# First block prepared in two token halves, loads in order of use, a third buffer of quantised activations, and the condition products two tiles later

## The chip, the cores and the metric

The kernel runs on one core of one Trainium2 chip. The metric is the device time of one execution in microseconds (us), median of the runs, lower is better. TensorE (PE) multiplies matrices, VectorE (DVE), ScalarE (ACT) and GpSimd (POOL) work on elements, and SyncE (SP) issues most of the DMA transfers. On-chip memory is SBUF; results of TensorE go to PSUM, which has eight banks of 128 x 512 fp32.

## The reference, cut to what matters

64 sequences of 64 tokens with 256 features (4096 tokens) pass through four layers, each steered by a condition vector of 64 numbers per sequence. The change touches the first layer and the preparation of the weights of the fourth.

```python
# layer 0: conditioned norm, gated GELU, ternary down product on quantised activations
scale = cond @ norm_w.T + 1.0
h = x * (scale[:, None, :] * rsqrt(mean(x * x) + EPS))
val, gate = split(h @ up_w.T)                 # 256 -> 2 x 1024
h = val * gelu(gate)
hq = clip(round(h * 127 / max|h|), -128, 127) / (127 / max|h|)   # per token
x = hq @ ternary(down_w).T + x                # 1024 -> 256
# layer 1: attention (16 heads) and SwiGLU, ada-rmsnorm with gamma, beta, alpha from cond
# layer 2: layernorm plus tanh(cond @ lin_w.T + lin_b)
# layer 3: low-rank adapter; its matrices are made for each sequence:
dWd = (h_lang @ Wdd.T + bdd) * 0.1            # 64 -> 128 x 256 per sequence
dWu = (h_lang @ Wdu.T + bdu) * 0.1
x = x + relu(x @ (Wd + dWd).T + bd) @ (Wu + dWu).T + bu
```

## The kernel before

The tokens are worked in 8 blocks of T = 512, each of TT = 4 tiles of 128 tokens. A product of fp32 precision is made of three TensorE products of high and low parts (`mm3`, L81 to L85): hi x hi, hi x lo, lo x hi. A "split" makes the high part on ScalarE (a rounding copy, L222 for x, L322 for the weights) and the low part on VectorE (L223, L326).

**Layer 0** runs in `l0`, a loop over n, the tile number. In iteration n stand: `upper(n, 0)` and `upper(n, 1)`, each 12 products of 128 x 512 for the two halves of the hidden features, followed by gelu on ScalarE (`g`, L408) and the gate product on VectorE (`h`, L409); then `quant(n)` on VectorE (L415 to L420: maximum, scale, round, write the bf16 tile `q`), a transpose of `q` to `qt` by a DMA on the SP queue (L422), and `lower(n - 3)`: eight bf16 products with the ternary weights (L434) and the residual sum on VectorE (`x`, L435). The tiles `q` have two buffers, `qt` four.

**The generated matrices** of layer 3 are made in the same loop. At n = 5, 8, 11, 15, 18, 22, 25 and 29 four pieces are made: `gen_load` brings a 512 KB piece of weights (`gt`, SP queue), `gen_make` multiplies it (L278), `gen_stage` copies two PSUM banks to an SBUF tile (`stg`, ScalarE, L291), `gen_store` sends it to DRAM from the POOL queue (L298). The staging tiles alternate between the pools "a" and "kv", two in each.

**Block preparation.** `prep_load(i)` loads x of block i feature-major (`xf`) and token-major (`xt`), `prep_parts(i)` scales it by the condition (`xs`, L371) and splits it (`xhl`, `xll`), `prep_scale(i)` makes the root of the mean square: squares on ScalarE (L215), the root on POOL (L206 to L208). For block i+1 these stand at the block's first, second and third tile.

**The start.** Up weights come in four pieces `upst0` to `upst3`. `warm` lets TensorE transpose an identity matrix while the loads run. The first products are those of tiles 0 and 1 with the weight pieces 2 and 0 (`first`, 24 products), in the order of the tiles.

**The other condition products.** `cond_norm` makes layer 0's scale at the start. The rest are made by two hooks: `cond_load` (the loads `cwt`, `vc`, `bo`) and `cond_rest` (an iota on POOL, 28 products L152 and 4 products L156, 14 VectorE instructions L138 to L170, two tanh on ScalarE, a store to `alphad`). Hooks of iteration n run after both `upper` of that iteration and, for n < 31, before `quant(n)`.

**What sets the order.** PE, ACT, DVE and POOL run in the order of the program text. The SP queue's DMAs are put in order by a scheduler. Tiles of one tag share a fixed number of buffers, and an instruction that writes a new tile waits until the old one in that buffer was read. PSUM is one ring of eight banks.

Of the kernel before, what the change touches and what calls it, by code (L numbers as in the profile page):

```python
# [8 lines left out]
F32 = mybir.dt.float32  # L9
F32R = mybir.dt.float32r  # L10
BF16 = mybir.dt.bfloat16
AF = mybir.ActivationFunctionType
ALU = mybir.AluOpType
# [4 lines left out]
P = 128  # L18
NB = 64
L = 64  # L20
D = 256
NTOK = NB * L
T = 512
NBLK = NTOK // T
BB = T // L
TT = T // P
FF = 1024
BN = 128
X1 = 5
# [3 lines left out]
V_NORM, V_AG, V_AB, V_AA, V_FG, V_FB, V_FA, V_LIN = range(8)  # L33
# [3 lines left out]
def tile_kernel(ctx: ExitStack, tc, xT, x, condT, cw, upT, downT, qkvT, woT, ghT, outT_w,  # L37
                vecs, rows, g1, g2, gb, out):
    nc = tc.nc
# [3 lines left out]
    main = ctx.enter_context(tc.tile_pool(name="main", bufs=1))  # L43
# [8 lines left out]
    pools = {}  # L52
# [7 lines left out]
    uid = [0]  # L60
# [13 lines left out]
    def block(name):  # L74
        return main.tile([P, TT, D], F32, tag="x1", bufs=X1, name=name)

    def tok(ap, i):

        return ap[i * T:(i + 1) * T, :].rearrange("(t p) d -> p t d", p=P)

    def mm3(out, l, r, first, last):  # L81

        nc.tensor.matmul(out, lhsT=l[0], rhs=r[0], start=first, stop=False)  # L83
        nc.tensor.matmul(out, lhsT=l[0], rhs=r[1], start=False, stop=False)  # L84
        nc.tensor.matmul(out, lhsT=l[1], rhs=r[0], start=False, stop=last)  # L85

    def b3(ap):
        return ap.rearrange("p (b l) -> p b l", l=L)
# [16 lines left out]
    cv = const.tile([P, 8, 2, NB], F32, name="cv")  # L105
# [1 line left out]
    w2 = const.tile([P, 2], F32, name="w2")  # L107
    par = const.tile([P, 2], F32, name="par")

    def bc(v, c, i):  # L110

        return cv[:, v, c, i * BB:(i + 1) * BB].unsqueeze(2).broadcast_to([P, BB, L])

    def cond_vector(cwv, pb, o=0):
        for c in range(2):
# [4 lines left out]
    def cond_norm():  # L120
        nc.vector.tensor_scalar(cv[:, V_NORM], cond_vector(cwn, bank("mm")), 1.0, None, ALU.add)
# [75 lines left out]
    def two(pool, name, kc, n):  # L197
        return [pool.tile([P, kc, n], F32R, name=f"{name}{k}") for k in range(2)]
# [12 lines left out]
    def rms(xb, name):  # L211
        ss = main.tile([P, TT], F32, tag="ss", bufs=2, name=f"ss{name}")
        for t in range(TT):
            junk = main.tile([P, D], F32, tag="junk", bufs=1, name=f"junk{name}_{t}")
            nc.scalar.activation(junk, xb[:, t], AF.Square, accum_out=ss[:, t:t + 1])  # L215
        return rsqrt(ss, 1.0 / D, 1e-6, name)

    def parts(name):
        return [main.tile([P, 2, T], F32R, tag=k, bufs=2, name=f"{k}{name}") for k in ("xh", "xl")]

    def split(hl, c, xs, eng=None):
        nc.scalar.copy(hl[0][:, c], xs)  # L222
        (eng or nc.vector).tensor_tensor(hl[1][:, c], xs, hl[0][:, c].bitcast(F32), ALU.subtract)  # L223
# [34 lines left out]
    GC = 512  # L258
    gen_left = [(g, sd, k) for g, sd in ((g1, s1d), (g2, s2d)) for k in range(16384 // (2 * GC))]
    gen_loaded, gen_made, gen_staged, gen_turn = [], [], [], []  # L260
# [21 lines left out]
    def gen_stage():  # L282
        if gen_made:
            pb, dst = gen_made.pop(0)
            uid[0] += 1

            gen_turn.append(pools["kv"] if len(gen_turn) % 2 else pools["a"])
            stg = gen_turn[-1].tile([P, 2, GC], F32, tag="stg" if len(gen_turn) % 2 else "qf", bufs=2,
                                    name=f"stg{uid[0]}")
            for s in range(2):  # L290
                nc.scalar.copy(stg[:, s], pb[s])  # L291
            gen_staged.append((stg, dst))
# [8 lines left out]
    def l0(hooks):  # L301
        pool = pools["a"]
        up = two(pool, "up", 2, 2 * FF)
# [3 lines left out]
        wm = sb[:, 1:2]  # L307
        blk, til = {}, {}

        ups = {}  # L310

        def load_up(j, *queues):

            js = slice(j * 512, (j + 1) * 512)
            ups[j] = main.tile([P, 2, 512], F32, tag="x1", bufs=X1, name=f"upst{j}")
            n = 2 // len(queues)
            for k, queue in enumerate(queues):
                cs = slice(k * n, (k + 1) * n)
                queue.dma_start(out=ups[j][:, cs], in_=upT.rearrange("(c p) n -> p c n", p=P)[:, cs, js])

        def half_hi(j, c):
            nc.scalar.copy(up[0][:, c, j * 512:(j + 1) * 512], ups[j][:, c])  # L322

        def half_lo(j, c):
            js = slice(j * 512, (j + 1) * 512)
            nc.vector.tensor_tensor(up[1][:, c, js], ups[j][:, c], up[0][:, c, js].bitcast(F32), ALU.subtract)  # L326
# [24 lines left out]

        def prep_load(i):
            xf = pool.tile([P, 2, T], F32, tag="xf", bufs=1, name=f"xf{i}")
            src = xT.rearrange("(c p) t -> p c t", p=P)[:, :, i * T:(i + 1) * T]
            if i == 0:
                for c in range(2):
                    nc.sync.dma_start(out=xf[:, c], in_=src[:, c])
                load_up(0, nc.sync, nc.scalar)
            else:
                nc.sync.dma_start(out=xf, in_=src)  # L360
            xt = block(f"xt{i}")
            nc.sync.dma_start(out=xt, in_=tok(x, i))
            blk[i] = [xt, xf, parts(f"l0_{i}"), None]

        def prep_parts(i):

            xf, hl = blk[i][1:3]
            xss = []
            for c in range(2):
                xs = main.tile([P, T], F32, tag="xg", bufs=2, name=f"xs{i}_{c}")  # L370
                nc.vector.tensor_tensor(b3(xs), b3(xf[:, c]), bc(V_NORM, c, i), ALU.mult)  # L371
                xss.append(xs)
            for c in range(2):
                yield
                split(hl, c, xss[c])

        def prep_scale(i):
            blk[i][1] = rms(blk[i][0], f"l0_{i}")

        def first(tiles):  # L380

            for n in tiles:
                til[n] = pool.tile([P, FF], F32, tag="h", bufs=2, name=f"h{n}")
                til[n, 0] = bank("up"), bank("up")
            for k, off in enumerate((FF, 0)):
                o = slice(off, off + 512)
                for c in range(2):
                    for n in tiles:
                        xh, xl = blk[n // TT][2]
                        ts = slice(n % TT * P, (n % TT + 1) * P)  # L390
                        mm3(til[n, 0][k], (xh[:, c, ts], xl[:, c, ts]), (up[0][:, c, o], up[1][:, c, o]), c == 0, c == 1)

        def upper(n, ch, part=None):
            i, t = divmod(n, TT)
# [17 lines left out]
        def quant(n):  # L412
            h = til[n]
            am = pool.tile([P, 4], F32, tag="am", bufs=5, name=f"am{n}")
            nc.vector.tensor_reduce(am[:, 0:1], h, AX.X, ALU.max, apply_absolute_value=True)  # L415
            nc.vector.tensor_scalar(am[:, 1:2], am[:, 0:1], 1e-5, 1.0 / 127.0, ALU.max, ALU.mult)
            nc.vector.reciprocal(am[:, 2:3], am[:, 1:2])
            nc.vector.tensor_scalar(h, h, am[:, 2:3], MAGIC, ALU.mult, ALU.add)
            q = pool.tile([P, FF], BF16, tag="q", bufs=2, name=f"q{n}")
            nc.vector.tensor_scalar(q, h, -MAGIC, 127.0, ALU.add, ALU.min)  # L420
            qt = pool.tile([P, 8, P], BF16, tag="qt", bufs=4, name=f"qt{n}")
            nc.sync.dma_start_transpose(out=qt, in_=q)  # L422
            til[n] = (am, qt)
# [16 lines left out]
        def warm(n):  # L440

            pb = bank("mm")
            for _ in range(n):
                nc.tensor.transpose(pb[:, :P], ident, ident)

        load_up(2, nc.scalar, nc.scalar)
        prep_load(0)
        nc.sync.dma_start(out=ct[64:128], in_=condT)
        load_up(3, nc.sync)
        load_up(1, nc.sync)  # L450
        til["ones"] = pool.tile([P, P], F32, name="ones")

        nc.scalar.activation(sa, nhalf[:, 0:2], AF.Gelu)
# [1 line left out]
        warm(12)  # L455
        half_hi(2, 0)
        cond_norm()
        warm(8)
        for c, _ in enumerate(prep_parts(0)):
            if c == 0:  # L460
                half_lo(2, 0)
            else:
                half_hi(2, 1)
        half_lo(2, 1)
        for c in range(2):
            half_hi(0, c)
            half_lo(0, c)
        prep_scale(0)
        first((0, 1))
        nc.vector.tensor_scalar(gl, ct, 0.1, None, ALU.mult)  # L470
        for j in (3, 1):
            for c in range(2):
                half_hi(j, c)
                half_lo(j, c)
        upper(0, 0, "rest")
        upper(1, 0, "rest")
        N = NBLK * TT
# [2 lines left out]
        for n in range(N + 2):  # L480
# [24 lines left out]
            if n == N - 1:  # L505
                quant(n)
# [430 lines left out]
    nc.gpsimd.memset(vx, 0.0)  # L937
    splits = Splitter(nc.vector, (qkv[0], qkv[1], qkvT, 2, 3 * D, 256), (wo[0], wo[1], woT, 2, D, 256))

    hooks = {3: [cond_load], 4: [cond_rest], 7: [splits.load]}  # L940
    for n in range(8, 16):
        hooks[n] = [splits.turn]
    last = NBLK * TT
# [25 lines left out]
    splits = Splitter(nc.gpsimd, (*pools["gh"], ghT, 2, 2 * FF, 512), (*pools["wout"], outT_w, 8, D, 256))  # L969
# [17 lines left out]
    for w in range(W):  # L987
        i, tp = divmod(w, 2)
# [87 lines left out]
    for n in range(5, N):  # L1076
        i, f = divmod(n, 8)
# [14 lines left out]
        up = i - 2 if more and f == 7 else i - 2 if not more and f == 0 else -1  # L1092
# [107 lines left out]
```

## Time and profile before

| | us |
|---|---|
| median of 3 runs | 771.09 (769.52 to 771.65) |
| the profiled execution | 768.89, span 767.1 |
| busy PE | 750.2 (98%) |
| busy DVE, ACT, POOL | 546.7, 396.3, 339.4 |
| moved by DMA | 118.87 MB, mean 155 GB/s |

The profile is of one execution; its times count from the start of the span. A row of the timeline gives the start, the duration, the engine, the line of the kernel, the operation, output <- inputs, the tile's shape, and in square brackets how long the engine stood idle before it and what ended that. SPq, POOLq and so on are the engines' sequencers, which issue DMAs. A row of the waits gives the sum, the number and the longest of the waits of one kind. Matmuls are pipelined, so a row's duration overlaps the next; the distance between starts is what counts. "Granted clock" is the share of full speed at which TensorE was allowed to run. A DMA's row in the timeline is its issue; its landing is later. In the chain of waits a DMA's piece runs from issue to landing.

Where the sections below speak of iteration n, these are starts in the profile of the kernel before: upper(1,1) 21.16, upper(5,0) 45.99, the generated products of n=5 48.98, upper(5,1) 52.75, upper(6,0) 56.45, upper(6,1) 59.34, upper(7,0) 62.95, upper(8,1) 76.01, upper(25,1) 207.98.

### The profile page before, as it was taken

Reading aid. Unit: us, or ns where it says so; the run is one execution under the profiler, and the core shown is the slowest. Engines: PE = TensorE matmul, PEld = TensorE weight load, DVE = VectorE, ACT = ScalarE, POOL = GpSimd, SP = SyncE. Lnnn points to the kernel's source line nnn. Section 1 sums busy time; section 2 is a strip of 40 time slices with the busy share of each in tenths; the row PEclk is TensorE's granted clock in tenths of the full one; section 3 lists DMA queues with packets and bytes.
Section 4 is the critical chain, followed back from the end, with each engine's and each line's share of the span. In section 5 each row is a group of like instructions: output and inputs, shape, how many; then the busy total and the mean of one; then the engine's idle time right before and its main releaser. Section 6 shows DMA issues by size and latency. Waiting matters only on the chain.

```text
span 767.1 us, 17409 instructions
## 1 busy us (share of the span) xinstructions
PE 750.2 (98%) x7034; PEld 618.9 (81%) x7034; DVE 546.7 (71%) x864; ACT 396.3 (52%) x818; POOL 339.4 (44%) x348
## 2 busy tenths in 40 slices
PE   8999999999899989999999999999999999999997
PEld 6866776676576878888888888888888888888886
DVE  4898777877587789998999886545555555555665
ACT  5434445435345378988878674535353434434232
POOL 2022223032224336676656417564646464545291
PEclk9999999999999999999999999999999999999999
DMA  8759998998986883555664137714180709070921
GB/s 299 200 128 255 315 279 175 334 257 191 266 211 140 184 188 88 139 143 141 157 153 110 45 125 179 165 28 112 40 181 24 197 3 218 1 192 2 232 45 56
DMA packets 117184, 118.87 MB, mean 155 GB/s; under 512 B 39616, under 2 KB 100672, under 8 KB 117104
## 3 DMA queue, kind: packets, MB, share of 16 engines
q1 hardware_dynamic: 109104, 91.55, 48.7%
q0 software_dynamic: 7488, 25.37, 10.7%
q8 instruction: 55, 0.90, 0.5%
q10 hardware_dynamic: 512, 0.85, 0.4%
q14 instruction: 25, 0.20, 0.1%
HBM read 71.41 MB, written 29.56 MB: 132 GB/s over the span
## 4 chain that ended last, share of the span: by engine, by line
PE 84%; DVE 7%; DMA 4%; issue 3%; ACT 1%; POOL 0%; SPq 0%; DVEq 0%; POOLq 0%; ACTq 0%
PE mm L83 10%; PE mm L84 10%; PE mm L85 10%; PE gh L83 7%; PE gh L84 7%; PE gh L85 7%; PE acc L83 4%; PE acc L85 4%; PE acc L84 4%; PE mm L278 3%; PE mm L434 3%; PE mm L632 2%; PE S L591 2%; PE mm L239 2%; DMA qt<-q 2%
## 5 line engine op out<-in xcount | busy, mean ns | idle before, releaser
L83 PE MATMUL mm<-up,xhl 128*128 128x512 f32 x256 | 106.4, 416 | 0.6 <-DVE h L409 0.5
L84 PE MATMUL mm<-up,xhl 128*128 128x512 f32 x256 | 103.0, 402 | 2.2 <-DVE up L326 2.2
L85 PE MATMUL mm<-up,xll 128*128 128x512 f32 x256 | 102.7, 401 | 0.0
L83 PE MATMUL gh<-xhf,gh 128*128 128x512 f32 x244 | 97.3, 399 | 0.0
L84 PE MATMUL gh<-xlf,gh 128*128 128x512 f32 x244 | 97.0, 397 | 0.0
L85 PE MATMUL gh<-xhf,gh 128*128 128x512 f32 x244 | 96.9, 397 | 0.0
L737 DVE TENSOR_TENSOR sg<-gh,sg 128x512 f32<-128x512 f32 x61 | 42.0, 688 | 77.1 <-ACT sg L736 39.9
L408 ACT ACTIVATE g<-mm,rs_l 128x512 f32<-128x512 f32 x64 | 43.7, 687 | 93.2 <-PE mm L85 60.3
L759 DVE TENSOR_TENSOR hlo<-sg,hhi 128x512 fp32r<-128x512 f32 x61 | 58.5, 959 | 31.2 <-ACT hhi L758 30.2
L758 ACT CAST hhi<-sg 128x512 fp32r<-128x512 f32 x61 | 37.8, 619 | 78.0 <-DVE sg L737 77.1
L409 DVE SCALAR_TENSOR_TENSOR h<-mm,rs_l,g 128x512 f32<-128x512 f32 x64 | 47.0, 746 | 41.8 <-PE mm L85 41.7
L83 PE MATMUL acc<-wout,hhi 128*128 128x256 f32 x256 | 75.1, 293 | 0.0
L85 PE MATMUL acc<-wout,hlo 128*128 128x256 f32 x256 | 72.7, 284 | 0.3 <-DVE hlo L759 0.2
L84 PE MATMUL acc<-wout,hhi 128*128 128x256 f32 x256 | 72.4, 283 | 0.0
L243 POOL TENSOR_TENSOR xg<-xg,cv 128x512 f32<-128x512 f32 x32 | 35.3, 1112 | 79.8 <-DVE xg L242 79.8
L83 PEld LDWEIGHTS mm<-up,xhl 128*128 128x128 f32 x256 | 49.2, 192 | 18.7 <-DVE h L409 3.6
L84 PEld LDWEIGHTS mm<-up,xhl 128*128 128x128 f32 x256 | 49.2, 192 | 12.8 <-DVE up L326 2.7
L85 PEld LDWEIGHTS mm<-up,xll 128*128 128x128 f32 x256 | 49.1, 192 | 12.2 <-DVE xll L223 0.3
L85 PEld LDWEIGHTS gh<-xhf,gh 128*128 128x128 f32 x244 | 46.1, 189 | 10.7
L84 PEld LDWEIGHTS gh<-xlf,gh 128*128 128x128 f32 x244 | 46.4, 190 | 8.1
L83 PEld LDWEIGHTS gh<-xhf,gh 128*128 128x128 f32 x244 | 46.4, 190 | 8.1
L736 ACT ACTIVATE sg<-gh 128x512 f32<-128x512 f32 x61 | 35.9, 589 | 29.2 <-PE gh L85 28.9
(189 smaller groups left out, 1886.7 us busy)
## 6 DMA issues: line engine op xcount, KB each, us to landing
gt<-in_g SPq DMA_DIRECT2D x32, 512.0 KB, 8.9
rows<-alphad SPq DMA_DIRECT2D x48, 256.0 KB, 4.3
s1d<-stg POOLq DMA_DIRECT2D x32, 256.0 KB, 9.6
s2d<-stg POOLq DMA_DIRECT2D x32, 256.0 KB, 6.6
vb<-vx SPq DMA_DIRECT2D x32, 256.0 KB, 4.6
wd<-s1d SPq DMA_DIRECT2D x32, 256.0 KB, 6.4
wu<-s2d SPq DMA_DIRECT2D x32, 256.0 KB, 6.4
xt<-in_x SPq DMA_DIRECT2D x8, 512.0 KB, 8.2
```

Source lines behind the costliest of these rows:

```text
L83: nc.tensor.matmul(out, lhsT=l[0], rhs=r[0], start=first, stop=False)
L84: nc.tensor.matmul(out, lhsT=l[0], rhs=r[1], start=False, stop=False)
L85: nc.tensor.matmul(out, lhsT=l[1], rhs=r[0], start=False, stop=last)
L243: nc.gpsimd.tensor_tensor(b3(xg), b3(xg), bc(vb, c, i), ALU.add)
L278: nc.tensor.matmul(pb[s][c * 64:(c + 1) * 64], lhsT=gl[h], rhs=gt[h, c * GC:(c + 1) * GC], start=True, stop=True, tile_position=(64 * s, 6 ...
L408: nc.scalar.activation(g, pg, AF.Gelu, scale=rs[:, t:t + 1])
L409: nc.vector.scalar_tensor_tensor(h[:, ch * 512:(ch + 1) * 512], pv, rs[:, t:t + 1], g, ALU.mult, ALU.mult)
L434: nc.tensor.matmul(py[:, :D], lhsT=qt[:, f, :], rhs=wq[:, f, :], start=f == 0, stop=f == 7)
L736: nc.scalar.activation(sg, pg, AF.Silu)
L737: nc.vector.tensor_tensor(sg, pv, sg, ALU.mult)
L758: nc.scalar.copy(h_hi, sg)
L759: nc.vector.tensor_tensor(h_lo, sg, h_hi.bitcast(F32), ALU.subtract)
```

## The change

It has three parts.

1. The start. Block 0 is loaded and prepared in two halves of 256 tokens (four sequences): the first half of both feature chunks comes first, then the weight piece `upst0`, `xt0`, `upst3`, `upst1`, and the second half of `xf`. `first` now goes by operand: for each weight piece and feature chunk, hi x hi of both tiles, then hi x lo, then lo x hi. `half_lo` of the weights stands between the low parts of x. Eight warm-up transposes become ten. The second half is prepared after weight piece 3 and before weight piece 1.
2. `cond_load` goes from n = 3 to n = 5, `cond_rest` from n = 4 to n = 6.
3. `q` gets a third buffer in pool "a". The staging tiles of pool "a" are moved to "kv": the even ones are the two halves of one 8 KB "kb" tile, the odd ones stay "qf" tiles.

On the queues this gives, as the two built programs show: SP issues after the start `xf` half 0, upst0, xt0, upst3, upst1, `xf` half 1, then the ternary weights and the `gt` as before. The two `cwt` loads were issued before the loop's sixth `gt` and now stand behind the transpose of tile 4; `bo` stands behind two more `gt` and `xf3`, as its buffer is one of block 2's `xs`. On POOL the iota stands behind block 2's root and no longer behind block 1's. In later parts of the program the order on every engine is the same.

```diff
+            k = len(gen_turn)
+            if k == 0:
+                gen_turn.append(pools["kv"].tile([P, 2, 2, GC], F32, tag="kb", bufs=2, name="stgs"))
+            else:
+                gen_turn.append(None)
+            stg = gen_turn[0][:, k // 2 % 2] if k % 2 == 0 else \
+                pools["kv"].tile([P, 2, GC], F32, tag="qf", bufs=2, name=f"stg{uid[0]}")
...
             if i == 0:
-                for c in range(2):
-                    nc.sync.dma_start(out=xf[:, c], in_=src[:, c])
-                load_up(0, nc.sync, nc.scalar)
+                H = T // 2
+                nc.sync.dma_start(out=xf[:, :, :H], in_=src[:, :, :H])
+                load_up(0, nc.sync, slice(0, 1))
+                load_up(0, nc.scalar, slice(1, 2))
+                nc.sync.dma_start(out=xt, in_=tok(x, i))
+                load_up(3, nc.sync)
+                load_up(1, nc.sync)
+                nc.sync.dma_start(out=xf[:, :, H:], in_=src[:, :, H:])
...
             for k, off in enumerate((FF, 0)):
                 o = slice(off, off + 512)
                 for c in range(2):
-                    for n in tiles:
-                        xh, xl = blk[n // TT][2]
-                        ts = slice(n % TT * P, (n % TT + 1) * P)
-                        mm3(til[n, 0][k], (xh[:, c, ts], xl[:, c, ts]), (up[0][:, c, o], up[1][:, c, o]), c == 0, c == 1)
+                    for x, w in ((0, 0), (0, 1), (1, 0)):
+                        for n in tiles:
+                            ts = slice(n % TT * P, (n % TT + 1) * P)
+                            nc.tensor.matmul(til[n, 0][k], lhsT=blk[n // TT][2][x][:, c, ts], rhs=up[w][:, c, o],
+                                             start=c + x + w == 0, stop=c + x == 2)
...
-            q = pool.tile([P, FF], BF16, tag="q", bufs=2, name=f"q{n}")
+            q = pool.tile([P, FF], BF16, tag="q", bufs=3, name=f"q{n}")
...
-        warm(8)
-        for c, _ in enumerate(prep_parts(0)):
-            if c == 0:
-                half_lo(2, 0)
-            else:
+        warm(10)
+
+        for c, _ in enumerate(prep_parts(0, slice(0, BB // 2))):
+            if c == 1:
                 half_hi(2, 1)
-        half_lo(2, 1)
+            half_lo(2, c)
         for c in range(2):
             half_hi(0, c)
             half_lo(0, c)
+        first((0, 1))
         prep_scale(0)
-        first((0, 1))
         nc.vector.tensor_scalar(gl, ct, 0.1, None, ALU.mult)
-        for j in (3, 1):
-            for c in range(2):
-                half_hi(j, c)
-                half_lo(j, c)
+        for c in range(2):
+            half_hi(3, c)
+            half_lo(3, c)
+        for _ in prep_parts(0, slice(BB // 2, BB)):
+            pass
+        for c in range(2):
+            half_hi(1, c)
+            half_lo(1, c)
...
-    hooks = {3: [cond_load], 4: [cond_rest], 7: [splits.load]}
+    hooks = {5: [cond_load], 6: [cond_rest], 7: [splits.load]}
```

More of the change, by code (lines that the diff above doesn't have):

```diff
@@ L108, in tile_kernel, with bc @@
     par = const.tile([P, 2], F32, name="par")
-    def bc(v, c, i):
-        return cv[:, v, c, i * BB:(i + 1) * BB].unsqueeze(2).broadcast_to([P, BB, L])
+    def bc(v, c, i, bs=slice(0, BB)):
+        n = bs.stop - bs.start
+        return cv[:, v, c, i * BB + bs.start:i * BB + bs.stop].unsqueeze(2).broadcast_to([P, n, L])
     def cond_vector(cwv, pb, o=0):
@@ L285, in gen_stage @@
             uid[0] += 1
-            gen_turn.append(pools["kv"] if len(gen_turn) % 2 else pools["a"])
-            stg = gen_turn[-1].tile([P, 2, GC], F32, tag="stg" if len(gen_turn) % 2 else "qf", bufs=2,
-                                    name=f"stg{uid[0]}")
+            k = len(gen_turn)
[5 more added lines that the diff above has]
+                pools["kv"].tile([P, 2, GC], F32, tag="qf", bufs=2, name=f"stg{uid[0]}")
             for s in range(2):
@@ L308, in l0, with load_up @@
         blk, til = {}, {}
[L310 to L319, printed above, removed]
+        ups, xfs = {}, {}
+        def load_up(j, queue, chunks=slice(0, 2)):
+            if j not in ups:
+                ups[j] = main.tile([P, 2, 512], F32, tag="x1", bufs=X1, name=f"upst{j}")
+            queue.dma_start(out=ups[j][:, chunks],
+                            in_=upT.rearrange("(c p) n -> p c n", p=P)[:, chunks, j * 512:(j + 1) * 512])
         def half_hi(j, c):
@@ L353, in prep_load, with prep_parts @@
             xf = pool.tile([P, 2, T], F32, tag="xf", bufs=1, name=f"xf{i}")
+            xt = block(f"xt{i}")
+            xfs[i] = xf
+            blk[i] = [xt, None, parts(f"l0_{i}"), None]
             src = xT.rearrange("(c p) t -> p c t", p=P)[:, :, i * T:(i + 1) * T]
             if i == 0:
-                for c in range(2):
-                    nc.sync.dma_start(out=xf[:, c], in_=src[:, c])
-                load_up(0, nc.sync, nc.scalar)
+                H = T // 2
[6 more added lines that the diff above has]
+                nc.sync.dma_start(out=xf[:, :, H:], in_=src[:, :, H:])
             else:
                 nc.sync.dma_start(out=xf, in_=src)
[L361 to L367, printed above, removed]
+                nc.sync.dma_start(out=xt, in_=tok(x, i))
+        def prep_parts(i, bs=slice(0, BB)):
+            xf, hl = xfs[i], blk[i][2]
+            ts = slice(bs.start * L, bs.stop * L)
             xss = []
             for c in range(2):
-                xs = main.tile([P, T], F32, tag="xg", bufs=2, name=f"xs{i}_{c}")
-                nc.vector.tensor_tensor(b3(xs), b3(xf[:, c]), bc(V_NORM, c, i), ALU.mult)
+                xs = main.tile([P, T], F32, tag="xg", bufs=2, name=f"xs{i}_{c}_{bs.start}")[:, ts]
+                nc.vector.tensor_tensor(b3(xs), b3(xf[:, c, ts]), bc(V_NORM, c, i, bs), ALU.mult)
                 xss.append(xs)
@@ L374, in prep_parts @@
                 yield
-                split(hl, c, xss[c])
+                nc.scalar.copy(hl[0][:, c, ts], xss[c])
+                nc.vector.tensor_tensor(hl[1][:, c, ts], xss[c], hl[0][:, c, ts].bitcast(F32), ALU.subtract)
         def prep_scale(i):
@@ L444, in warm @@
                 nc.tensor.transpose(pb[:, :P], ident, ident)
-        load_up(2, nc.scalar, nc.scalar)
+        for c in range(2):
+            load_up(2, nc.scalar, slice(c, c + 1))
         prep_load(0)
         nc.sync.dma_start(out=ct[64:128], in_=condT)
-        load_up(3, nc.sync)
-        load_up(1, nc.sync)
         til["ones"] = pool.tile([P, P], F32, name="ones")
@@ L467, in l0 @@
             half_lo(0, c)
+        first((0, 1))
         prep_scale(0)
-        first((0, 1))
         nc.vector.tensor_scalar(gl, ct, 0.1, None, ALU.mult)
-        for j in (3, 1):
-            for c in range(2):
-                half_hi(j, c)
-                half_lo(j, c)
+        for c in range(2):
[3 more added lines that the diff above has]
+            pass
+        for c in range(2):
+            half_hi(1, c)
+            half_lo(1, c)
         upper(0, 0, "rest")
```

## The prediction

> **What bounds the kernel now.** I read the page's first section, then the table of busy time by stretch, then the waits, and last the timeline and the chain around the two places where TensorE stands still.
>
> ```profile
> PE 750.2 (98%) x7034; PEld 618.9 (81%) x7034; DVE 546.7 (71%) x864; ACT 396.3 (52%) x818; POOL 339.4 (44%) x348
> ```
> ```profile
> 0.00:20.00 20.00, 16.41 (x56) 12.83 (x57) 9.34 (x16) 10.31 (x23) 3.85 (x11) 1.00 0.89 302
> 20.00:60.00 40.00, 39.49 (x219) 29.63 (x218) 36.56 (x71) 18.15 (x37) 6.27 (x10) 1.00 0.67 174
> 100.00:200.00 100.00, 100.00 (x536) 73.46 (x535) 75.20 (x136) 42.14 (x88) 26.43 (x41) 1.00 0.98 253
> 200.00:213.00 13.00, 11.03 (x62) 6.15 (x61) 4.01 (x10) 5.49 (x10) 2.82 (x4) 0.87 1.21 234
> ```
> Columns: stretch, length, busy PE, PEld, DVE, ACT, POOL, then granted clock, DMA share, GB/s. TensorE is the bound almost everywhere, so an edit pays only where PE stands still or runs slowly: 3.6 us missing in 0 to 20, 2.0 us in 200 to 213, and the half clock there (0.87). From 20 to 60 VectorE is full too (36.56 of 40): there PE can run ahead no further than VectorE frees PSUM banks.
>
> ```profile
> DVE q L420 <- DMA qt<-q: 3.7, 1, 3.7
> PE mm L278 <- DVE x L435: 2.9, 2, 2.0
> PE mm L84 <- DVE up L326: 2.2, 1, 2.2
> ```
> Each is (nearly) one event. The last is the start:
> ```profile
> 7.21 0.79 PE L83 MATMUL mm<-up,xhl 128*128 128x512 f32 x1
> 8.80 0.69 DVE L371 TENSOR_TENSOR xs<-xf,cv 128x512 f32<-128x512 f32 x1 [2.30 <-DMA xf<-in_xT]
> 10.15 0.80 PE L84 MATMUL mm<-up,xhl 128*128 128x512 f32 x1 [2.15 <-DVE up L326]
> 15.19 0.63 PE L83 MATMUL mm<-up,xhl 128*128 128x512 f32 x1
> 16.26 0.39 PE L83 MATMUL mm<-up,xhl 128*128 128x512 f32 x1
> 21.43 0.75 DVE L409 SCALAR_TENSOR_TENSOR h<-mm,rs_l,g 128x512 f32<-128x512 f32 x1 [2.05 <-PE mm L85]
> ```
> The first product runs at 7.21. The second needs the low part of the weights, which VectorE has queued behind the scaling of x's second chunk, and that chunk lands at 8.78. Matmuls start 0.427 us apart until 16.01 and 0.233 after. The 24 products of `first` end at 18.36.
>
> The other two waits are one stall, in the chain:
> ```profile
> 189.24 15.79 DMA qt<-q
> 205.12 0.69 DVE q L420
> 206.04 0.49 DVE x L435
> 206.58 1.47 PE mm L278 x8
> ```
> Tile 24's q needs one of two q buffers, held by tile 22's transpose, which took 15.79 us to land. VectorE waits 3.65 us; behind it in order stands L435, which frees the bank for the last generated products. PE idles 204.43 to 206.58, then runs at half clock:
> ```profile
> 208.57 0.63 PE L84 MATMUL mm<-up,xhl 128*128 128x512 f32 x1
> 210.64 0.39 PE L83 MATMUL mm<-up,xhl 128*128 128x512 f32 x1
> ```
>
> **The change part by part.** The profiled execution took 768.89 us (span 767.1, 1.8 around it), 2.2 under the median of 771.09. The steps are worked out on its trace; I subtract their sum from the median, as the waits are the program's own.
>
> *Half block first.* Before, PE had x's first chunk at 5.71. Now 256 KB with 256 tokens of both chunks come first. The Trainium skill (DMA: Bandwidth & Descriptors, "Queues, rings and completion order") says that an engine takes turns between queues packet by packet, which speaks against this: rows are now 1 KB, and the ACT queue's upst2 has 2 KB packets. In this trace a 1 KB packet takes 46 ns and a 2 KB one 84, so 16 turns of (46+84) replace 8 of (84+84): 0.74 us later, 6.45. By bytes alone it is 5.8. I take 6.2. Then scaling 256 wide 0.4 (L435, 256 wide, is 0.40 to 0.49), conversion 0.42 (ACT's 256-wide square), so PE starts near 7.1 to 7.5. The two extra warm-up transposes (0.21 each) end by 7.6 at most and fill that wait. lo(2,0) comes 1.0 us after the scaled c0 (xs c1 0.4, itself 0.6) and is wanted after two cold matmuls (0.85); no more 2.15 wait. upst0 lands near 10.2 as before and is wanted after 12 matmuls, about 12.4. So PE runs on from about 7.4.
>
> The clock rose at 16.01 and later changed at 207.16 and 210.57; all lie on a 3.413 us grid, so a step was also at 12.60. Before, the stretch 9.19 to 12.60 held idle time to 10.15; now it is full. I take 12.60: 12 matmuls at 0.427 and 12 at 0.233 from 7.4 make 15.4, against 18.36 (-2.9). If the clock still waits until 16.01, 20 cold and 4 warm end at 16.9 (-1.5). By the DMA rule (start 0.4 later) about 0.2 less.
>
> Next late: weights 1 and 3. ACT does the squares of xt0 (to 13.79), two conversions for weight 3 (1.08), two 256-wide of x's second half (0.84), two for weight 1 (1.08): 16.8, VectorE's last low part near 17.5. The second half of upper(0,1) wants it at 17.5: 0 to 0.5 us of wait. upper(1,1) begins near 18.5 (21.16 before): PE gains 2.6. VectorE's row of 21.43 comes near 19.3: it gains 2.1, having four more instructions (each 512-wide pair became four 256-wide) and a later gelu. As VectorE is full until 55.9, PE is held to about 2.0 by n=6.
>
> *Condition products from n=4 to n=6, their loads from n=3 to n=5.* The same work moves: PE 28 x L152 (2.00 us) and 4 x L156 (0.65), about 2.5 net; VectorE 14 instructions, 46.51 to 50.14, 3.63; ACT two tanh; POOL an iota and alphad's store; SP's cwt x2 (448 KB), vc, bo. PE reaches it at the end of upper(6,1): before 62.1, less 2.5 moved, less 2.0, is 57.6. The queues that it is moved past:
> ```profile
> 32.80 0.13 POOL L136 IOTA part<- 128x1 int32 x1
> 63.80 0.19 POOL L206 TENSOR_SCALAR ms_l<-ssl 128x4 f32<-128x4 f32 x1 [8.52 <-ACT junkl L215]
> 53.40 2.36 SPq L422 DMA_TRANSPOSE qt<-q  x1
> ```
> On SP, cwt now stands behind tile 4's transpose. That landed at 63.44, 14.46 us after the generated products of n=5 began (48.98). These begin near 43.4 now (less 2.5, 2.6 and a 0.5 us wait at 45.99), so it lands near 57.8; 448 KB at some 2 us per 512 KB (two gt landed 1.3 to 2.0 apart here), partly beside it, is 1.1 to 1.75: cwt at about 59. That is a new wait s at PE of about 1.4, between 0 (cwt beside the transpose) and 3. Behind it in PE's order stand lower(3) and upper(7,0), so all of PE.
>
> On POOL the iota stood after block 1's root; now it is behind block 2's, which ended at 65.10, 5.8 us after upper(6,1) began (59.34): 54.8 + 5.8 = 60.6. VectorE's 14 instructions begin with its result, 1 to 2 us after VectorE is free. bo now lies behind two gt and xf3, which before landed 4.65 us after that transpose: about 64.0 with cwt ahead; L166, 2.3 us into the 14, wants it at 62.9, a further 1.0. Behind both in VectorE's order stand quant(6) and L435 of tiles 3 and 4, which free PE's banks. From the iota: 3.63 + 1.0, quant(6) 3.1, L435 0.72, two h 1.43, quant(7) 3.04, L435 of tile 4 0.79, together 13.7: 74.3, and with the last generated bank behind it upper(8,1) at 75.2. By PE's own path it is 76.01 - 1.95 + s. Before: 76.01. So the gain left is the smaller of 0.8 and 1.95 - s: 0.55 with s at 1.4, 0.8 with 1.1, -1 with 3; with bo and iota in time 1.8. I take 0.8. A wait above 2 us would add a half-clock window (below).
>
> *Third q buffer.* q(24) then waits for tile 21's transpose, long landed, and PE first needs transpose 22 in lower(22) near 208.3, 3.3 us after it landed; 23 (landed 206.18) near 214.7. What goes is 2.15 us of PE idle. The Trainium skill (TensorE: Matmul & The Clock Gate, "Why this matters for your kernels") sets the harmful gap at over some 3 us, which would leave 2.15 alone. The trace shows a half-clock window of 3.41 us after this gap: half of it, 1.6, goes too. Sum 3.75, against 2.15 by the rule. Another view agrees: iteration 22 (same work) took 10.30 us and 25 took 14.02, 3.72 more. The trace decides: 3.7. Floor 0: transpose 22 later by over 3.3.
>
> *Staging.* Same four places in rotation, the same store to wait for; only addresses change. Attention's first use of that "kb" place follows the last store by over 20 us. I put nothing: what hides it is that ACT copies four stagings after the store; without that cover a copy waits for one store's landing (9.6 us in the page's list), against the 23 us between the visits at n=5 and n=8 (48.98 to 72.44).
>
> Sum: 0.8 + 3.7 = 4.5, profiled 764.4, median 766.6.
>
> **The rivals.** (1) cwt, iota and bo are in time: 1.8 + 3.7 = 5.5, 765.6; if VectorE holds PE back less than I think, 2.6 + 3.7 = 6.3, 764.8. For: at 20 to 60 us the DMA engines are busy 0.67 only; against: the one queue order. (2) The start's gain is used up at n=6 to 8: only the buffer is left, 767.4, or 768.9 if only 2.15 of it. (3) The third buffer doesn't pay, as transpose 22 slips or another takes its place (DMA share 0.98 in 100 to 200): 0.8 alone, 770.3. That the halves don't help (first half near 6.5, clock at 16.01) costs 1.1 to 1.4 of gain and falls in (2). (4) Slower: cwt behind a long transpose. If tile 4's, issued near 47.7 (53.40 less 3.63 and 2.1), needs 15.8 as tile 22's did, it lands at 63.5 and cwt at 65.0: PE idles 7.4, plus 1.6 of half clock, less 1.95 and 3.7: +3.35, 774.4. It decides from a wait of 6.4 us (cwt at 64.0) on; against: the same transpose took 10.04 in this trace.
>
> **How the numbers follow.** 0.3% or 2.3 us is about what a measurement of this kernel can tell from no change. Forecast 0.40, (1) 0.25, (2) 0.13, (3) 0.15, (4) 0.07. Faster: forecast, (1) and nearly all of (2), 0.75; same: (3) and a rest, 0.18; slower 0.07. The range goes from 763.8 (rival 1 with 1 us more) to 770.6 (beyond rival 3).
>
> **What would show it.** PE without a gap from 7.5, `first` ending near 15.4, clock full at 12.6; a PE wait at L152 for cwt near 57.6, and VectorE waits for the iota and for bo; upper(8,1) near 75.2; no wait at q L420 and no half clock near 205, and what follows earlier by 4 to 5 us. Wrong if L152 waits over 3 us, if lower(22) waits for its transpose, or if a new wait stands in 213 to 270, where the stretch lost 0.9 before.

## The result and the profile after

The change made the kernel slower: 773.56 us, median of 7 runs (773.14 to 775.75), against 767.58 (766.15 to 771.65) for the kernel before measured beside it, a ratio of 1.0081 with a 95% interval of 1.0058 to 1.0104. The kernel before is 3.5 us lower here than in the first three of these runs, which the prediction started from, so differences and ratios are compared below, not absolute times. The forecast was 4.5 us faster.

In the changed kernel's text the lines have moved: L152 is now L153, L420 is L432, L434 is L446, L371 is L381, the products of `first` are L402. Its busy time by stretch, with the same columns as before:

```profile
0.00:20.00 20.00, 16.49 (x62) 13.11 (x63) 8.94 (x20) 10.36 (x24) 3.85 (x11) 1.00 0.89 298
20.00:60.00 40.00, 38.73 (x191) 27.99 (x189) 36.96 (x65) 20.09 (x43) 5.80 (x8) 1.00 0.65 151
60.00:100.00 40.00, 35.43 (x188) 26.05 (x189) 23.93 (x52) 11.37 (x23) 8.80 (x15) 0.87 0.85 254
200.00:213.00 13.00, 13.00 (x77) 9.26 (x79) 10.00 (x18) 3.14 (x6) 2.71 (x5) 1.00 1.20 256
```

The hole that was at 200 to 213 (11.03 busy, clock 0.87) is closed: 13.00 of 13.00 at full clock. A new one stands at 58 to 74: TensorE has 35.43 of 40 in 60 to 100, and there the mean clock is 0.87. The start, 0 to 20, has not gained (16.49 busy against 16.41). The waits name both places:

```profile
PE mm L153 <- DMA cwt<-in_cw: 5.7, 2, 5.3
DVE gl L480 <- DMA ct<-in_condT: 2.7, 1, 2.7
```

There is no row for q L432 any more. The timeline of TensorE around the hole, and below it the chain of waits into it:

```profile
58.49 0.40 PE L85 MATMUL mm<-up,xll 128*128 128x512 f32 x1
...
64.24 0.65 PE L153 MATMUL mm<-ct,cwt 64*128 64x64 f32 x2 [5.35 <-DMA cwt<-in_cw]
65.22 3.25 PE L153 MATMUL mm<-ct,cwt 64*128 64x64 f32 x26 [0.33 <-DMA cwt<-in_cw]
68.40 1.12 PE L157 MATMUL mm<-cwt,ct 64*64 64x256 f32 x4
69.45 1.89 PE L446 MATMUL mm<-wq,qt 128*128 128x256 bf16 x8
70.99 0.78 PE L83 MATMUL mm<-up,xhl 128*128 128x512 f32 x1
```
```profile
51.94 2.42 SPq L132
54.41 10.67 DMA cwt<-in_cw
```

TensorE is done with upper(6,1) at 58.7, and the two cwt loads land at 64.1 (51.94 plus 12.2, the tile's landing time) and 65.08. The price is more than the idle time. The windows show the clock:

```profile
58.70:63.40 4.70, 0.19 (x1) 0.00 (x0) 2.68 (x10) 1.53 (x6) 1.31 (x3) 1.00 1.03 264
63.40:73.70 10.30, 9.13 (x47) 7.14 (x48) 4.96 (x13) 0.52 (x2) 0.69 (x1) 0.50 0.81 218
73.70:80.00 6.30, 6.30 (x33) 4.99 (x32) 4.14 (x7) 1.38 (x2) 2.02 (x3) 1.00 0.64 158
```

For 10.3 us TensorE had half its clock, and the small products L153, L157, lower(3) and the first of upper(7,0) fell into it. From 64.24 to upper(7,0) in the chain (71.34) are 7.1 us, where the same work takes 2.5 + 0.9 at full clock in the profile before: 3.7 lost; 71.34 to 73.7 at half clock loses 1.2. With 5.5 us of idle time the stop costs 10.4. Against this stands what the start still saves at that point, 0.9. The sum, 9.5, fits the profiles: lower(4) and what follows are 9.3 us later than before. The third q buffer takes 3.7 of these back near 204, and the profile's span is 5.2 us longer (772.3 against 767.1).

### The profile page after: what moved, and what is told of

Its sections match the earlier page's. It is cut to its first block, busy times and chain, and to the rows that moved or that the text cites. A ratio compares the mean times of both kernels' runs of the same rounds, so it can differ in the third digit from the quotient of the medians.

```text
span 772.3 us, 17418 instructions
## 1 busy us (share of the span) xinstructions
PE 752.5 (97%) x7036; PEld 620.2 (80%) x7036; DVE 547.1 (71%) x868; ACT 396.5 (51%) x820; POOL 339.3 (44%) x348
## 4 chain that ended last, share of the span: by engine, by line
PE 83%; DVE 4%; DMA 2%; issue 2%; ACT 1%; SPq 1%; POOL 0%; DVEq 0%; ACTq 0%
PE mm L83 10%; PE mm L85 9%; PE mm L84 9%; PE gh L83 7%; PE gh L84 7%; PE gh L85 7%; PE acc L83 4%; PE acc L85 4%; PE acc L84 4%; PE mm L279 3%; PE mm L446 3%; PE mm L646 2%; PE S L605 2%; PE mm L240 2%; PE mm L665 2%
## 5 line engine op out<-in xcount | busy, mean ns | idle before, releaser
L83 PE MATMUL mm<-up,xhl 128*128 128x512 f32 x248 | 102.0, 411 | 0.1
L84 PE MATMUL mm<-up,xhl 128*128 128x512 f32 x248 | 98.6, 398 | 0.2 <-DVE up L328 0.2
L85 PE MATMUL mm<-up,xll 128*128 128x512 f32 x248 | 98.4, 397 | 0.0
L420 ACT ACTIVATE g<-mm,rs_l 128x512 f32<-128x512 f32 x64 | 43.8, 688 | 93.4 <-PE mm L85 53.9
L83 PEld LDWEIGHTS mm<-up,xhl 128*128 128x128 f32 x248 | 47.1, 190 | 17.1 <-DVE x L447 1.7
L85 PEld LDWEIGHTS mm<-up,xll 128*128 128x128 f32 x248 | 46.9, 189 | 11.4
L84 PEld LDWEIGHTS mm<-up,xhl 128*128 128x128 f32 x248 | 47.0, 190 | 10.2 <-DVE up L328 0.5
```

The lines of the kernel that those rows point to most:

```text
L420: nc.scalar.activation(g, pg, AF.Gelu, scale=rs[:, t:t + 1])
```

## The experiments

First each part by itself, and the change with part 2 undone, on one chip beside the kernel before.

**The change with the condition products put back (e1).**
```diff
-    hooks = {5: [cond_load], 6: [cond_rest], 7: [splits.load]}
+    hooks = {3: [cond_load], 4: [cond_rest], 7: [splits.load]}
```


> The changed kernel with the condition products' hooks put back (load at n=3, work at n=4); the new start, the third q buffer and the moved staging stay. Theory A (the loss is part 2 alone: cwt waits on SP's queue behind tile 4's transpose): no wait at L153, the start's gain of about 2 us and the buffer's 3.7 us are left, 5 to 6 us faster than before. Theory B (the new start shifts the stores and transposes against each other, so that a long transpose hurts wherever it lies): not faster than before, a wait of several us somewhere between 45 and 100 us.

Measured: 766.78 us, ratio 0.9997 (0.9976 to 1.0017). The slowdown is gone, so it came with part 2. But 5 to 6 us were expected to be won, and nothing was: both theories missed in part. Its profile has two waits. At the start VectorE waits for ct, and in tile 18's `lower` TensorE waits for a transpose that took 18.6 us to land:

```profile
DVE gl L480 <- DMA ct<-in_condT: 3.8, 1, 3.8
PE mm L446 <- DMA qt<-q: 3.2, 1, 3.2
```

The second wait need not be in every execution: the profiled one, 770.09 us, was the slowest of the 14.

**The third buffer and the staging alone (e2)**, that is the kernel before with part 3.
```diff
-            q = pool.tile([P, FF], BF16, tag="q", bufs=2, name=f"q{n}")
+            q = pool.tile([P, FF], BF16, tag="q", bufs=3, name=f"q{n}")
...
```
The lines left out are those of the staging tiles, as in the change.

> The kernel before with only the third q buffer and the moved staging. Theory A: the wait at q L420 near 205 and the half-clock stretch behind it go, 3.7 us faster than before. Rival: transpose 22 is as late, lower(22) waits for it on TensorE, within 0.5 us of before.

Measured: 765.78 us, ratio 0.9975 (0.9959 to 0.9991), which is 1.9 us faster. In its profile the stretch 200 to 213 is full at full clock:

```profile
200.00:213.00 13.00, 13.00 (x77) 8.39 (x76) 7.62 (x15) 7.21 (x13) 2.39 (x4) 1.00 1.05 313
```

and lower(22) comes 3.9 us earlier than in the profile before. The mechanism holds; the median won only half of the 3.7 us that the one profile had shown. The kernel before ran from 764.2 to 773.6 us on this chip, and not every execution need hold that stall; that was not tested.

**The condition products alone (e3)**, that is the kernel before with the hooks at 5 and 6.
```diff
-    hooks = {3: [cond_load], 4: [cond_rest], 7: [splits.load]}
+    hooks = {5: [cond_load], 6: [cond_rest], 7: [splits.load]}
```


> The kernel before with only the condition products moved (load at n=5, work at n=6). Theory A: TensorE waits for cwt at L152 for 3 to 6 us and loses some 4 us more to half clock, 6 to 10 us slower than before, less up to 3.7 if the shift takes the stall near 205 away. Theory B (only in company with the new start): within 1 us of before.

Measured: 774.15 us, ratio 1.0103 (1.0064 to 1.0142). The same hole at the same place, without the new start and with two q buffers (whose stall, 4.4 us, is still there):

```profile
PE mm L152 <- DMA cwt<-in_cw: 5.7, 2, 5.5
DVE q L420 <- DMA qt<-q: 4.4, 1, 4.4
```

**The new start alone (e4)**, that is the change with parts 2 and 3 undone.

> The kernel before with only the new start (halves, load order, products by operand). Theory A: first ends 2 to 3 us earlier, the clock is full one 3.4 us step earlier, and about 2 us of it are left at the end; 2 us faster, if the stall near 205 stays as it is. Theory B: the gain is given back by a later wait, within 0.5 us of before.

Measured: 767.92 us, ratio 1.0006 (0.9988 to 1.0024): nothing won. The three parts give +0.06%, +1.03% and -0.25%, together +0.84%; the change measured +0.81%. Within their intervals the parts add up, and part 2 is the loss. VectorE's wait at the start is here too:

```profile
14.94 0.20 DVE L476 TENSOR_SCALAR gl<-ct 128x64 f32<-128x64 f32 x1 [3.73 <-DMA ct<-in_condT]
15.79 0.50 PE L84 MATMUL mm<-up,xhl 128*128 128x512 f32 x1 [1.02 <-DVE up L324]
```

Next: why is cwt late? Two kernels tell cwt's place on the SP queue from the slowness of what stands ahead of it.

**cwt and bo in the space of the ternary weights (e5).** In the change they are new tiles of tags whose buffers come free only around n = 5. The ternary weights' tile is free from n = 2. Hooks and the order of the engines stay.
```diff
-        bo = crest["bo"] = main.tile([NB, D], F32, tag="xg", bufs=2, name="bo")
+        bo = crest["bo"] = crest["wd"][1][:NB, 0]
-        cwt = crest["w"] = main.tile([P, 4, D], F32, tag="x1", bufs=X1, name="cwt")
+        cwt = crest["w"] = crest["wd"][0]
...
             wd, ones = til.pop("wd"), til.pop("ones")
+            crest["wd"] = wd
```


> The changed kernel, with cwt and bo loaded into the space of the ternary weights (free since n=2) in place of new tiles of 'x1' and 'xg'. Hooks and the order on PE, DVE, ACT and POOL stay; on SP the scheduler then puts cwt and bo ahead of tile 2's transpose, so that neither stands behind tile 4's. Theory A (cwt's place on the queue is the loss): cwt lands before 50 us, TensorE's wait of 5.7 us and the half clock of 10 us at L153 go, VectorE waits for the iota alone (about 1 to 2 us), 8 to 9 us faster than the changed kernel, 2 to 4 us faster than before. Rival (any late hook costs it, through the iota and the longer VectorE chain): 3 us or more are still lost between 58 and 85 us.

Measured: 765.42 us, ratio 0.9984 (0.9971 to 0.9997). That is 7 us faster than the change by the ratios (8 to 9 expected) and 1.2 faster than before (2 to 4 expected). The hole is gone, and TensorE goes through the 28 products in 2 us:

```profile
58.98 2.00 PE L153 MATMUL mm<-ct,wd 64*128 64x64 f32 x28
```

Tile 4's transpose is as slow here as in the change (12.1 us against 13.1), but cwt was issued at 34.1, ahead of it. VectorE's wait for the iota is left, 0.9 us, and TensorE loses 0.3 at the next generated products. The late hook as such is nearly free; cwt's place on the queue was the loss.

**The first stores held back (e7).** cwt stays behind tile 4's transpose, but the eight 256 KB stores of the first generated pieces go out together at n = 7.
```diff
                     gen_load()
-                    gen_store()
+                    if n > 6:
+                        gen_store()
+                if n == 7:
+                    for _ in range(3):
+                        gen_store()
```


> The changed kernel, with the eight 256 KB stores of the first four generated pieces (n=5 to 7) issued together at n=7; nothing else. Theory A' (the transpose of tile 4 took 13 us because its packets run beside the stores' packets; alone a transpose takes 3 to 4 us): it lands near 54, cwt near 56, in time for L153 at 58.5, no wait there, and 8 us faster than the changed kernel, less what the stores then cost at n=7 and 8. Rival (the queue order by itself: cwt has to wait for two gt and a transpose in any case): cwt lands after 60, still 2 us or more of wait.

Measured: 771.37 us, ratio 1.0074 (1.0046 to 1.0103), but with the loss in another place. Tile 4's transpose landed 4.4 us after its issue (13.1 in the change), cwt 4.4 to 4.6 after its own, and TensorE does not wait at L153. Where the stores are now, tile 7's transpose takes 12.2 us, the four loads of generated weights behind it land 11.7 to 12.4 us after issue, and TensorE falls to 17.73 of 20. There the chain goes through a staging copy on ScalarE, which had to wait for a store that took 9.2 us to land:

```profile
70.00:90.00 20.00, 17.73 (x96) 10.97 (x95) 7.06 (x14) 7.13 (x13) 10.24 (x17) 1.00 1.05 269
```

The DMA queues of the two kernels, packets, megabytes and share of the 16 engines' time, in the stretch in which the transpose and what follows it are on the way; first the change (52 to 60 us), then e7 (48.6 to 54), where the second queue has no row:

```profile
q1 hardware_dynamic: 992, 0.27, 56.1%
q0 software_dynamic: 256, 0.82, 51.8%
```
```profile
q1 hardware_dynamic: 1391, 1.46, 106.2%
```

In the change the engines are fully busy for 8 us and move 1.1 MB; in e7 they move 1.5 MB in 5.4. For comparison a transpose that has the engines to itself, in the kernel before from 40.8 to 43.9 us:

```profile
q1 hardware_dynamic: 1056, 0.26, 44.1%
```

From these rows (share times 16 engines times the stretch, over the packets) a packet of the transpose's queue took 72 ns on average in the change and 21 ns alone. A store packet took 259 ns in the change, and 156 ns in a stretch with stores alone (the change, 249 to 251 us: 183 packets, 89.1%). So packets of the two kinds stretch each other when they run together. Both things are needed for the hole: a transpose that shares its time with stores (e7 takes that away), and cwt behind it on the same queue (e5 takes that away).

Then the start.

**ct loaded early (e9)**, on e1.
```diff
                 nc.sync.dma_start(out=xf[:, :, :H], in_=src[:, :, :H])
+                nc.sync.dma_start(out=ct[64:128], in_=condT)
...
-        nc.sync.dma_start(out=ct[64:128], in_=condT)
```


> The kernel e1 (new start, third buffer, condition products in their old place), with the second half of ct loaded behind x's first half and no longer behind x's second half. Theory A'' (VectorE's wait for ct at gl, 2.7 to 3.8 us, is what eats the start's gain): no wait at gl, low parts of weight 3 from 12.5 to 13, upper(1,1) 1 to 1.5 us earlier than in e1, the time 1 us faster than e1. Rival: the chain of ScalarE (squares of xt0, then weights 3 and 1) holds TensorE as much, nothing is won.

Measured: 765.54 us, ratio 0.9987 (0.9974 to 1.0). That is 1.2 us less than e1's median, but on another chip, and the ratios differ by less than their intervals: a gain in time is not shown. The wait at gl is gone, and upper(1,1) starts at 17.82 (19.06 in e1, 20.04 in the change, 21.16 before). Yet at lower(0) only 1.4 us of these 3.3 are left, less than the 2.1 in e1's profile.

Nor does the early ct always help. In the profiles of e10 and e11 below, which have it too, upper(1,1) starts at 18.73 and 18.33: ScalarE waited 1.5 and 1.2 us for xt0, its squares stand ahead of the conversions of weights 3 and 1, and TensorE lost 2.1 us behind these. That is the rival of this experiment. From e10:

```profile
11.09 0.42 ACT L217 ACTIVATE junkl<-xt 128x256 f32<-128x256 f32 x1 [1.48 <-DMA xt<-in_x]
16.74 0.50 PE L83 MATMUL mm<-up,xhl 128*128 128x512 f32 x1 [0.81 <-ACT up L325]
```

**All three mends (e8)**: e5, ct early, and the iota made at the start.

> The changed kernel with three mends: cwt and bo in the ternary weights' space, the second half of ct loaded early, the iota made at the start. Theory A: none of the waits at L153, at the iota and at gl; start's gain of 2 to 3 us and the third buffer's 1.9 us stay, 4 us faster than before. Rival (what is won at the start is given back at the first long transpose): within 1.5 us of e2, that is 1 to 2 us faster than before.

Measured: 765.0 us, ratio 0.9974 (0.9957 to 0.9991); it was measured again beside e10:

> The mended kernel e8 once more, for the comparison with e10 on the same chip: 1 to 2.5 us faster than before, as in its first measurement (0.9974).

and gave 764.92, 0.9968 (0.9952 to 0.9984). That is the rival's figure, no more than the third buffer alone, but not at a long transpose, as the rival had it. The start's gain of 3.6 us at upper(1,1) (17.59) went into a wait of VectorE for block 1's x, for which TensorE then waits in its turn at upper(5,0):

```profile
25.48 1.29 DVE L384 TENSOR_TENSOR xs<-xf,cv 128x512 f32<-128x512 f32 x2 [2.49 <-DMA xf<-in_xT]
41.00 0.50 PE L83 MATMUL mm<-up,xhl 128*128 128x512 f32 x1 [1.66 <-DVE h L424]
```

`xf` has one buffer. Its next load waits until block 0's second half has been scaled. It was issued at 11.10 before and at 14.61 here, behind the first four loads of generated weights and xt1.

**A second buffer for xf (e10, and again e13)**, on e8.
```diff
-            xf = pool.tile([P, 2, T], F32, tag="xf", bufs=1, name=f"xf{i}")
+            xf = pool.tile([P, 2, T], F32, tag="xf", bufs=2, name=f"xf{i}")
```


> The mended kernel e8 with two buffers for xf, so that block 1's load no longer waits until block 0's second half is scaled; on SP it now stands ahead of the first generated weights. Theory A (VectorE's wait of 2.5 us for xf1 at the scaling of block 1 takes back the start's gain, 3.6 us at upper(1,1) but 1.1 us at lower(0) and after): no wait there, lower(1) 1 to 2 us earlier than in e8, and the time 1 to 2 us faster than e8. Rival (VectorE is full up to 55 us anyway, and holds TensorE at the same place): within 0.5 us of e8.

Measured: 761.51 us, ratio 0.9929 (0.9911 to 0.9947). That is 3.4 us faster than e11, more than the 1 to 2 expected. Its profiled execution was a long one (span 765.9), with TensorE waiting 1.4 us, until 175.0, for a transpose of 16.8 us, so it was run once more:

> The kernel e10 once more beside e12, with a second profile: 5 to 6 us faster than before. If the start's gain is what came through, lower(3) stands 2 to 3 us earlier than in before and the rest is the third buffer's; if not, more is gained after 100 us.

Measured: 761.61 us, ratio 0.9928 (0.9899 to 0.9957). From 20 to 60 TensorE is busy without a break, as in e10's first profile:

```profile
20.00:60.00 40.00, 40.00 (x224) 29.50 (x223) 37.42 (x73) 19.30 (x44) 7.03 (x10) 1.00 0.83 198
```

lower(3), behind the moved condition products, starts at 58.33 against 62.14 before; these 3.8 us stay to 200, and near 204 another 3.7 come. In e10's first profile the gain at lower(3) is 2.6. This kernel is 5.5 us faster than the kernel before, which the measurement can tell, and so faster than the change.

**The second xf buffer without the new start (e12)**, on e2.

> The kernel e2 (before, with the third q buffer) with two buffers for xf, old start and old place of the condition products. Theory A (the second xf buffer pays because it lets the new start's gain through): no faster than e2, 1 to 2 us faster than before. Rival (it pays by itself, as every block's load of x goes out earlier and nearer to the transposes' quiet stretches): 4 us or more faster than before, as e10.

Measured: 765.78 us, ratio 0.9981 (0.9962 to 0.9999), as e2. So the buffer by itself gives nothing that can be told; in e10 it lets the start's gain through. e10 holds the new start and the late condition products together, and no run has the second buffer with the new start alone.

## Why the prediction was wrong

The step that failed is the wait s in the step on the condition products. It was put between 0 and 3 us, with 1.4 as the likeliest and 1.6 for the half clock only above 2. TensorE stood idle for 5.5 us, and the half clock behind that cost 4.9. A second step failed at the start, "Next late: weights 1 and 3", and took most of the gain that was to pay for it.

**The condition products at n = 6.** The place, the queue and the order were right: TensorE came to L153 at 58.7 (57.6 said), cwt was behind tile 4's transpose, and all of TensorE stood behind it. The size was wrong. The sum took the transpose to land 14.46 us after the generated products began, as in the profile before. They began at 44.5 (43.4 said), and the transpose landed at 62.7, 18.2 after: it was issued 0.6 us later behind them, and took 13.1 us to land where the profile before had 10.0. The second cwt load came 2.4 us after the transpose (1.2 said). So s was 6.4 by the sum's own terms, and 3.7 of the 5.0 too little lie in that interval, which was no constant. With stores beside it tile 4's transpose took 10.0 us before, 12.1 in e5, 13.1 in the change and 13.4 in e3, and 4.4 without them in e7; why it ranges from 10.0 to 13.4 with them is open. The half clock, put at 1.6, lasted 10.3 us. The iota (forecast 60.6, came at 61.7) was the limit only where cwt was in time (e5). bo (64.0 said) landed at 69.3 and held nobody up only because VectorE came to L167 at 70.3. Besides, by its own rule the sum gave 0.55 with s at 1.4, and it took 0.8. The prediction's own sign of being wrong, a wait over 3 us at that line, is what came.

**The first block.** That TensorE would run on without its 2.15 us stop was right. The terms were off. The first half landed 4.8 to 7.0 us after its issue at 1.37 in the kernels with the new start, so at 6.2 to 8.4, where I had bounded it by 5.8 and 6.45; in the change's own profile it was 8.4, and TensorE began at 9.39 (forecast 7.4) and ended `first` at 16.41 (forecast 15.4). The full clock came near 12.2 (12.6 said). My estimate of 0.74 us for the 1 KB packets came from the rule of turns packet by packet (the Trainium skill, DMA: Bandwidth & Descriptors, "Queues, rings and completion order"), and took each 1 KB row as one packet, where the page has some 9 to 17 descriptors in one; no kernel here separates the packets' part from the rest of the spread.

In the step on weights 1 and 3 I priced the instructions of ScalarE and called the load order "in order of use", but did not follow every DMA that it moved. The second half of ct, issued at 3.81 before, was issued at 8.39 after the change and landed 6.5 us later; VectorE's `gl` needs it, and behind `gl` stand the low parts of weights 3 and 1. upper(1,1) began at 20.04: 1.1 us gained, not 2.6. Of the 1.5 that are missing, 1.0 is the late end of `first`; in upper(0,1) TensorE then stood still for another 0.8, where 0 to 0.5 was said. In e1, with a wait of 3.8 us at `gl`, these 0.8 are 1.9, and in e9, without that wait, 0.5. A third thing was missed: block 1's load of x is released by the scaling of block 0's second half, which now comes late (e8, e10).

**The rival that came true.** Rival 4, given 0.07, had the mechanism: cwt behind a long transpose, landing at 65.0, 3.35 us slower. Measured: 65.08, and 6.0 us slower. It idled less than said (5.5 against 7.4) and lost more to the clock. That cwt landed within 0.1 us of the rival's figure is luck: the transpose was issued 1.9 us later than it said and took 2.7 less. I had dismissed it since "the same transpose took 10.04 in this trace", although the same trace held one of 15.79. With transposes of 3, 8, 10 and 16 us in one trace, a single value should not have set a bound of 3 us on s.

**The third buffer.** Right in its mechanism and, in the profile, in its size: what was 9.3 us late before 204 is 5.5 late after, 3.7 forecast. In the median it is worth 1.9 (e2), half. Of rule (a harmful gap of over some 3 us; the Trainium skill, TensorE: Matmul & The Clock Gate, "Why this matters for your kernels") and trace at that place, the trace was right about the clock: the shorter hole had cost a half-clock stretch as well. The profile's rows have the hole at 1.97 us idle, not 2.15, and 3.41 us at half clock cost 1.7, not 1.6; the sum is the same.

**The staging** cost nothing that shows; no kernel tried it apart from the buffer.

**Left open.** Why the clock stayed at half for 10.3 us in the change, about as long in e3, and only 3.4 in the profile before, was not tried: the small products and the holes between them fill that time, but no run varied them. The middle third of that stretch was counted busy throughout, with parts of L153 and lower(3) and all of L157 in it, and yet the last third was at half clock too:

```profile
66.81:70.23 3.42, 3.42 (x22) 2.35 (x21) 1.70 (x4) 0.52 (x2) 0.00 (x0) 0.50 1.06 232
```

Whether the move of the condition products gives anything once cwt is in time was not measured by itself: e8, which has it with the iota made early, differs from e9, which has not, by less than the interval.

## What to carry to other kernels

When loads are put in "order of use", list every load that moves back and the first instruction that needs it; a small one (16 KB of ct) can hold an in-order engine. Before a load is moved behind another transfer on one queue, take the longest landing of that transfer in the trace as its price, and remember that an idle TensorE can pay again in its clock (here after gaps of 2.0, 3.2 and 5.4 us, not after one of 1.7). And look where the new load's buffer comes free: a tile in dead space, or a second buffer, moved cwt and xf ahead without any change to the order of the work.

## What the runs showed of the hardware

I had not expected that a DMA transpose and stores from the POOL queue slow each other that much: tile 4's transpose of 256 KB landed in 4.4 us without stores beside it (e7), and in 10.0 to 13.4 with them (before, the change, e3, e5), while the engines were busy all the time and in the change moved as little as 1.1 MB in 8 us. Stores beside a transpose do not always cost that much: tile 18's landed in 5.2 us in the profile before and in 18.6 in e1's, with stores in both. Nor that a half-clock stretch would outlast its cause by so long: after 5.35 us of idle time the clock stayed at 0.50 for 10.3 us, although TensorE was counted busy for 9.13 of them.
